# Attention block after group norm: the last output projections in two parts, conversions on ScalarE, residuals one chain ahead

## The chip, the cores and the metric

The kernel runs on one core of a Trainium2 chip as one launch. The metric is the device time of one execution in microseconds (us); lower is better. The five engines run their own instruction queues in order[...]: PE (TensorE, matrix products), ACT (ScalarE), DVE (VectorE), POOL (GpSimd) and SP (SyncE, which here issues nearly all DMAs).

## The reference: what is computed

The input x is 4 images of 512 channels by 48x48 = 2304 positions, in float32. The rest is one self-attention block with a residual:

```python
hn = group_norm(x)                         # 32 groups of 16 channels, per image
qkv = einsum('oc,bchw->bohw', qkv_w, hn) + qkv_b      # 1536 x 512 weights
q, k, v = split(qkv.reshape(b, 3, 8, 64, 2304).astype(float16))
w = softmax(einsum('bhct,bhcs->bhts', q * scale, k * scale))
a = einsum('bhts,bhcs->bhct', w, v).astype(float32)
out = einsum('oc,bchw->bohw', proj_w, a) + proj_b     # 512 x 512 weights
return x + out
```

## The kernel before

**Units.** Of the two paths in the file only `fast_path` runs (`general_path` is entered if the softmax sums leave a safe range; a flag that the fast path computes at its end decides it). The 8 heads of an image are taken as 4 pairs, so there are 16 pairs g = 0..15, four for each image b. The 2304 positions are cut into five blocks j (`QBLOCKS`): four of 512 and one of 256. For each pair and block the keys are gone through in steps; one step k covers three sets of score matrices (`BURST = 3`) and is called an *item* here. A 512-block has six items, the 256-block three, a pair 27, the whole kernel 432 (`stream`, numbered n = 0..431 below).

**An item.** The main loop at the end of `fast_path` takes the items in order. It issues the scores of item n (PE, line 902, into three PSUM banks pairs of the pool `ps_s`), three exponentials of 128x1024 (ACT, line 909), the running sum of the exponentials of item n-1 (DVE, `add`, line 960), and the product with v of item n-2 (PE, line 927; `BEHIND = 2`). When a block is complete, PE adds up the softmax sums (`add_up`, line 980), DVE copies them out (990), SP sends them to another layout (`sums`, 994), DVE inverts them (1025), SP writes the inverse to DRAM (1027) and spreads it back over the partitions (1037), and POOL multiplies (`divide`, 1044). The result `att` is float16.

**Work beside the stream.** Everything else is cut into pieces that are put into one list, `beside`, in an order written out by hand: chains of matmuls that make q and k (`qk_chain`, 704), v (`v_chain`, 749) and the output projection (`proj_pieces`, 829). A chain fills one PSUM bank; all chains share the single bank of the pool `ps_w`, so DVE must empty it (713, 757, 849) before the next chain's matmuls may start. `fill(n)` issues pieces once for each item. How many it may issue is ruled by a credit that is raised by the work left over the items left up to the pair that needs it, and a piece waits in the list until its item `after` has come (`put_convert` and `put_proj`, with `ready` items after the end of the block). Pieces never overtake each other. Because the loop runs when the program is built, the result is a fixed order of instructions on each engine.

**Projection.** For a block of an image the four att tiles are first converted to float32 (`att32`: POOL, line 823; DVE for the last two blocks of the last pair), into one buffer for each of four chunks (`a32_0` to `a32_3`). Then for each 128 output channels one chain runs: four pairs times two halves of the weights (`whi`, `wlo`), eight matmuls into the shared bank. The 256-block has two chains of sixteen. DVE adds bias and the residual x (849), into the tile r that SP loaded (`residual`, 799), and SP stores it (856) one item later. r has three buffers (tag `res`); the load for chain k+1 is a piece of its own ahead of chain k.

**Images.** The projection of image b runs during the pairs of image b+1; that of the last image begins during the last pair, and its last two blocks with a part of the third run after the last item. Tiles of the normed x of the next image are loaded into the buffers of the present one as they come free (`reload`), with statistics and normalization as DVE tasks (`tasks`, up to two or four for each item, `do_tasks`). One block, (1, 3), has buffers elsewhere (`SPARE`) and is loaded early.

Of the kernel before, what the change touches and what calls it, by code (L numbers as in the profile page):

```python
# [467 lines left out]
def fast_path(  # L468
# [13 lines left out]

    const = ctx.enter_context(tc.tile_pool(name="const", bufs=1))
# [3 lines left out]
    apool = ctx.enter_context(tc.tile_pool(name="apool", bufs=8))  # L487
# [12 lines left out]
    SPARE = (1, 3)  # L500

    def load_x(b, j, c, engine):

        o, n = QBLOCKS[j]
        name = f"x_{b}_{c}_{j}"
        if (b, j) == SPARE:
            t = work.tile([P, n], F32, tag=f"a32_{c}", bufs=1, name=name)
        else:
            t = xpool.tile([P, n], F32, tag=f"x{c}_{j}", name=name)
        engine.dma_start(t, x[b, bass.ts(c, P), o : o + n])  # L510
        hn[b, c, j] = t
# [45 lines left out]
    def load_wproj(c):  # L557
        wproj[c] = work.tile([P, C], F32, tag="res", bufs=3, name=f"wproj_{c}")
        nc.sync.dma_start(wproj[c], proj_wT[bass.ts(c, P), :])
# [15 lines left out]
    fine = const.tile([P, 2, QB // P], F32, name="fine")  # L575
# [6 lines left out]
    def chain_bank(name):  # L582
        if alone[0]:
            return ps_s.tile([P, 2, QB], F32, tag="ps", name=name)[:, 0, :]
        return ps_w.tile([P, QB], F32, tag="pw", name=name)
# [202 lines left out]
    def residual(b, j, chunks):  # L788
        n = QBLOCKS[j][1]
        if at_end(b, j):  # L790

            tag = f"x{chunks[0]}_{j - NQ + 2}"
            xt = xpool.tile([P, QB], F32, tag=tag, name=f"r_{b}_{j}_{chunks[0]}")
        else:
            xt = work.tile(
                [P, QB], F32, tag="res", bufs=3, name=f"r_{b}_{j}_{chunks[0]}"
            )
# [4 lines left out]
    def at_end(b, j):  # L802

        return b == B - 1 and j >= NQ - 2

    def att32(b, j, pairs=range(NC)):
        o, n = QBLOCKS[j]
        if (b, j) not in at32:
            if at_end(b, j):
                at32[b, j] = [  # L810
                    xpool.tile([P, n], F32R, tag=f"x{c}_{j}", name=f"a32_{b}_{j}_{c}")
                    for c in range(NC)
                ]
            else:
                at32[b, j] = [
                    work.tile(
                        [P, QB], F32R, tag=f"a32_{c}", bufs=1, name=f"a32_{b}_{j}_{c}"
                    )[:, :n]
                    for c in range(NC)
                ]  # L820
        for c in pairs:
            engine = nc.vector if direct(b * NPAIR + c, j) else nc.gpsimd
            engine.tensor_copy(at32[b, j][c], atts[b * NPAIR + c][:, o : o + n])  # L823

    def proj_chain(b, j, m, ps):
        n = QBLOCKS[j][1]
        for c in range(NC):
            for i, w in enumerate((whi, wlo)):
                nc.tensor.matmul(  # L829
                    ps[:, :n],  # L830
                    w[:, c, bass.ts(m, P)],
                    at32[b, j][c],
                    start=(c == 0 and i == 0),
                    stop=(c == NC - 1 and i == 1),
                )

    def proj_pieces(b, j):


        n = QBLOCKS[j][1]  # L840

        def run(chunks):
            bank = chain_bank(f"pr_{b}_{j}_{chunks[0]}")
            places = [bank[:, i * n : (i + 1) * n] for i in range(len(chunks))]
            for m, ps in zip(chunks, places):
                proj_chain(b, j, m, ps)
            xt = res.pop((b, j, chunks[0]))
            for i, m in enumerate(chunks):
                nc.vector.scalar_tensor_tensor(  # L849
                    xt[:, i], places[i], bproj[:, m : m + 1], xt[:, i], ALU.add, ALU.add  # L850
                )

            loads.append(
                (
                    now[0] + 1,
                    lambda: nc.sync.dma_start(rows_of(out, b, j, chunks), xt),
                )
            )

        def ahead(k):  # L860
            if k < len(proj_list) and not at_end(b, proj_list[k][0]):
                residual(b, *proj_list[k])

        convert = [
            piece(0.0, lambda: att32(b, j, (NC - 1,) if at_end(b, j) else range(NC)))
        ]
        chains = []
        for k, (jj, chunks) in enumerate(proj_list):
            if jj != j:
                continue  # L870
            chains.append(
                [piece(0.0, lambda k=k: ahead(k)) for k in ([0] if k == 0 else [])]
                + [piece(0.0, lambda k=k: ahead(k + 1))]
                + [piece(QB / 290.0, lambda chunks=chunks: run(chunks), True, True)]
            )
        return convert, chains
# [35 lines left out]
    def values(u):  # L912
# [21 lines left out]
        if last:  # L934
            avx[g, j] = work.tile([P, QB], F32, tag="avx", name=f"avx_{g}_{j}")
            nc.vector.tensor_copy(avx[g, j][:, :n], av[0][:, :n])  # L936

    def direct(g, j):

        return g == NG - 1 and j >= NQ - 2  # L940

    def add(u):
# [6 lines left out]
        if direct(g, j) and (last or j == NQ - 1):  # L949
# [16 lines left out]
    def add_up(g, j):  # L966
# [3 lines left out]
        sl = ps_av.tile([P, QB], F32, tag="av", name=f"sl_{g}_{j}")  # L970
# [6 lines left out]
        for i, (t, r, a) in enumerate(steps):  # L977
            for h in range(2):
# [7 lines left out]
                )  # L986

        def rows():
            sx = work.tile([P, QB], F32, tag="rows", name=f"slx_{g}_{j}")
            nc.vector.tensor_copy(sx[:, :n], sl[:, :n])  # L990

            sm = small.tile([P, 2, QB // P], F32, tag="sums", name=f"sums_{g}_{j}")
            for h in range(2):
                nc.sync.dma_start(sm[:, h, : n // P], sx[h * D : h * D + 1, :n])
            sums[g, j] = sm
            return sx

        if direct(g, j):
            source = rows() if n == QB else sl
            inv = work.tile([P, QB], F32, tag="rows", name=f"inv_{g}_{j}")  # L1000
            nc.vector.reciprocal(inv[:, :n], source[:, :n])
            engine = nc.vector if source is sl else nc.gpsimd
            engine.tensor_tensor(
                atts[g][:, o : o + n], avx.pop((g, j))[:, :n], inv[:, :n], ALU.mult
            )
            if source is sl:
                rows()
        else:
            rows()

    def check_sums(g, j):
        n = QBLOCKS[j][1]
        sm = sums[g, j][:, :, : n // P]
        ok = fine[:, :, : n // P]
# [44 lines left out]
    def put_run(run, *args, when=None):  # L1059

        put([piece(0.05, lambda: run(*args), when=when)])

    def reload(b, j):


        def run():
            load_block(b, j)
            for c in range(NC):
                tasks.append((now[0] + 3, lambda c=c: stats(b, j, c)))
            if j == NQ - 1:  # L1070

                tasks.append((now[0] + 3, lambda: aggregate(b)))
                tasks.append((now[0] + 3, lambda: group_scale(b)))
                tasks.append((now[0] + 3, lambda: coefficients(b)))
                for jj in range(NQ):
                    for c in range(NC):
                        tasks.append((now[0] + 3, lambda jj=jj, c=c: normalize(b, jj, c)))
# [7 lines left out]
    def do_tasks(room):  # L1085
# [3 lines left out]
        while tasks and tasks[0][0] <= n and room > 0:  # L1089
            tasks.popleft()[1]()  # L1090
            room -= 1
# [18 lines left out]
    def ready(b, j):  # L1110
# [3 lines left out]
        return BEHIND + (2 if j >= NQ - 2 else 5)  # L1114
# [5 lines left out]
    def put_proj(b, j, *which):  # L1120

        end = ends[((b + 1) * NPAIR - 1) * NQ + j]
        for i in which or range(len(projs[b, j][1])):
            put(projs[b, j][1][i], end + ready(b, j) + 1)

    for b in range(B):
        g = b * NPAIR
        old = b - 1
        if b == 0:
# [7 lines left out]
            put_run(reload, *SPARE)  # L1137
        put_qk(g + 2, 1)
        put_qk(g + 2, 0)

        late = SPARE[1] if b == 0 else None
        last_tiles = [i for i in range(0, NT, 2) if i * P // QB == late]
        put_v(b, 1, [i for i in range(0, NT, 2) if i not in last_tiles])
        if b == B - 1:
            put_qk(g + 3, 1)
            put_qk(g + 3, 0)
            put_convert(old, 0)
            for j in range(NQ):
                put_proj(old, j)
                if j + 1 < NQ:  # L1150
                    put_convert(old, j + 1)
            for j in range(NQ - 2):
                put_convert(b, j)
                put_proj(b, j)
                if j < 2:
                    for jj, chunks in proj_list:
                        if jj == NQ - 2 + j:
                            put_run(residual, b, jj, chunks)
                    put_run(att32, b, NQ - 2 + j, range(NC - 1))
            put_convert(b, NQ - 2)  # L1160
            put_proj(b, NQ - 2)
            continue

        for j in range(NQ):
            if j == late:
                continue
            if j == 3 and b > 0:
                put_convert(old, 0)
# [3 lines left out]
        if late is not None:  # L1172
            put_v(b, 1, last_tiles)
            put_qk(g + 3, 1, (late,))
            put_qk(g + 3, 0, (late,))
# [55 lines left out]
    def fill(n):  # L1231
# [6 lines left out]
        do_tasks(  # L1238
            (2 if idle else 0)
            if ended(n - 1)  # L1240
            else (2 if idle else 1) if ended(n - BEHIND - 1) else 4 if idle else 2
        )
        rate, work = 0.0, 0.0
        for us, _, _, _, _, _, need in beside:
            work += us
            left = min(need * per_pair, len(stream)) - n
# [12 lines left out]
    def wanted(g):  # L1259

        while any(p[6] <= g for p in beside):
            while loads:
                loads.popleft()[1]()
            while tasks:
                tasks.popleft()[1]()
# [4 lines left out]
    end = len(stream)  # L1270
    for n in range(end):
# [103 lines left out]
```

## Time and profile before

| What | us |
|---|---|
| Median of 3 runs (lowest to highest) | 1649.59 (1648.8 to 1651.96) |
| The profiled execution, its own time | 1654.24 |
| Its span, from first to last instruction | 1652.5 |
| Start of the first item's scores | 80.6 |
| Start of item 395 (the last chain that makes q) | 1484.1 |
| Start of the scores of the last item | 1621.98 |
| End of the last exponential | 1625.3 |
| End of the last DVE addition | 1645.8 |

The profiled execution is one run; its time is 4.65 us above the median of the timed runs, of which 1.74 us lie outside its span. Sums are made inside the span and carried over to the median as a difference. The mean granted clock of TensorE is 0.996 of full speed. Busy times of PE count matmuls that overlap, with modelled ends, so idle PE time in a busy column understates waiting; the starts of the instructions do not have that fault, and stretches are measured by them.

### The profile page before, as it was taken

The page shows a single profiled execution, that of the slowest core. Times are in us where ns is not written, and L with a number is a line of the kernel's source. Part 1 is how long each engine was busy: PE and PEld are TensorE (multiplying, and loading weights), DVE is VectorE, ACT ScalarE, POOL GpSimd, SP SyncE. Part 2 cuts the span into 40 slices and gives each one's busy share as a digit, 9 for nine tenths or more (in the row PEclk, how much of TensorE's full clock was granted, in tenths as well). Part 3 has the DMA queues.
Part 4 walks back from the last instruction along what each step waited for, and adds up shares of the span by engine and source line. Part 5 has one row for each costly group of instructions (what it writes and reads, how often), then busy time and mean ns, then how long its engine had stood idle before and what let it go on. Part 6 is the DMA issues. An engine that isn't in the chain of part 4 may idle for free.

```text
span 1652.5 us, 28302 instructions
## 1 busy us (share of the span) xinstructions
PE 1591.0 (96%) x11500; PEld 695.2 (42%) x11500; DVE 1137.5 (69%) x1296; ACT 1247.7 (76%) x1317; POOL 372.1 (23%) x497
## 2 busy tenths in 40 slices
PE   6999999899999999899999999899999999999887
PEld 2533444343333534445333353345533334435445
DVE  5267668876666679786666666788667666767664
ACT  3077777788888888678887888667878888887772
POOL 1001111222121223413212121332211122214341
PEclk9999999999999999999999999999999999999999
DMA  7001012000000015421000001342100000013443
GB/s 217 1 14 40 11 40 71 17 14 11 14 18 14 15 36 147 120 70 37 14 15 11 14 18 55 109 132 74 37 14 11 14 17 15 15 29 107 134 122 124
DMA packets 95185, 82.11 MB, mean 50 GB/s; under 512 B 51140, under 2 KB 61252, under 8 KB 95044
## 3 DMA queue, kind: packets, MB, share of 16 engines
q1 hardware_dynamic: 93572, 79.14, 17.3%
q8 instruction: 92, 1.51, 0.4%
q10 hardware_dynamic: 1344, 1.05, 0.2%
q14 instruction: 49, 0.40, 0.1%
q0 software_dynamic: 128, 0.01, 0.0%
HBM read 60.70 MB, written 19.17 MB: 48 GB/s over the span
## 4 chain that ended last, share of the span: by engine, by line
PE 86%; DMA 5%; DVE 4%; POOL 2%; issue 2%; ACT 1%; SPq 1%; DVEq 0%; POOLq 0%
PE pqk L704 28%; PE ps L902 17%; PE av L927 17%; PE pv L749 15%; PE pr L829 6%; DMA out_dram<-r 2%; DVE acc L960 1%; PE ps L704 1%; PE sl L980 1%; POOL a L823 1%; DMA r<-x_dram 1%; ACT p L909 1%; DMA ib<-row 1%; DMA x<-x_dram 1%; DMA sums<-slx 1%
## 5 line engine op out<-in xcount | busy, mean ns | idle before, releaser
L909 ACT ACTIVATE p<-ps 128x1024 f16<-128x1024 f32 x1296 | 1232.7, 1027 | 361.9 <-PE ps L902 361.1
L960 DVE TENSOR_TENSOR acc<-acc,p 128x3072 f16<-128x3072 f16 x270 | 486.9, 1803 | 75.8 <-ACT p L909 75.4
L704 PE MATMUL pqk<-x,wqkv 128*64 128x512 f32 (+1 forms) x2464 | 519.3, 551 | 0.0
L902 PE MATMUL ps<-q,k 64*128 64x512 f16 (+1 forms) x2880 | 360.7, 359 | 10.8 <-ACT p L909 10.4
L927 PE MATMUL av<-p,v 128*64 128x512 f16 (+1 forms) x2880 | 360.7, 364 | 0.0
L1018 POOL TENSOR_SCALAR in<-sums 128x8 f32<-128x8 f32 (+1 forms) x160 | 121.3, 758 | 716.0 <-DMA sums<-slx 709.3
L749 PE MATMUL pv<-wqkv,x 128*64 128x256 f32 x2304 | 268.9, 380 | 4.3 <-DVE x L655 2.7
L704 PEld LDWEIGHTS pqk<-x,wqkv 128*64 128x64 f32 x2464 | 169.1, 137 | 223.5 <-issue 166.6
L1044 POOL TENSOR_TENSOR att<-avx,ib 128x512 f16<-128x512 f32 (+1 forms) x78 | 131.2, 1683 | 447.3 <-DMA ib<-row 396.9
L902 PEld LDWEIGHTS <-k 64*128 64x128 f16 x2880 | 106.6, 94 | 293.1 <-issue 246.4
L927 PEld LDWEIGHTS <-v 128*64 128x64 f16 x2880 | 131.7, 109 | 209.8 <-issue 164.8
L749 PEld LDWEIGHTS pv<-wqkv,x 128*64 128x64 f32 x2304 | 160.3, 137 | 97.5 <-issue 5.5
L829 PE MATMUL pr<-a,whi 128*128 128x512 f32 (+1 forms) x320 | 127.2, 405 | 23.1 <-DVE r L849 11.3
L960 DVE TENSOR_TENSOR acc<-p,p 128x3072 f16<-128x3072 f16 x79 | 138.2, 1749 | 0.0
L963 DVE TENSOR_TENSOR acc<-acc 128x1024 f16<-128x1024 f16 x156 | 115.3, 739 | 5.3
L829 PE MATMUL pr<-a,wlo 128*128 128x512 f32 (+1 forms) x320 | 118.4, 378 | 0.0
L713 DVE TENSOR_SCALAR q<-pqk,bqkv 128x512 f16<-128x512 f32 (+1 forms) x79 | 55.0, 696 | 86.6 <-PE pqk L704 86.3
L757 DVE TENSOR_TENSOR v<-pv,bv 128x512 f16<-128x512 f32 x72 | 49.8, 691 | 79.5 <-PE pv L749 79.2
L713 DVE TENSOR_SCALAR k<-pqk,bqkv 128x512 f16<-128x512 f32 (+1 forms) x75 | 52.2, 695 | 72.0 <-PE pqk L704 71.9
L849 DVE SCALAR_TENSOR_TENSOR r<-pr,bproj,r 128x512 f32<-128x512 f32 (+1 forms) x80 | 54.9, 694 | 61.9 <-PE pr L829 43.3
L936 DVE COPY avx<-av 128x512 f32<-128x512 f32 (+1 forms) x80 | 51.0, 637 | 66.8 <-PE av L927 66.5
L829 PEld LDWEIGHTS pr<-a,whi 128*128 128x128 f32 x320 | 60.9, 190 | 65.1 <-POOL a L823 23.1
(51 smaller groups left out, 453.3 us busy)
## 6 DMA issues: line engine op xcount, KB each, us to landing
r<-x_dram SPq DMA_DIRECT2D x72, 256.0 KB, 3.0
out_dram<-r SPq DMA_DIRECT2D x72, 256.0 KB, 3.1
ib<-row SPq DMA_DIRECT2D x126, 128.0 KB, 3.0
x<-x_dram SPq DMA_DIRECT2D x62, 256.0 KB, 4.4
x<-x_dram SPq DMA_DIRECT2D x16, 128.0 KB, 4.6
sums<-slx SPq DMA_DIRECT2D x128, 2.0 KB, 2.0
ib<-row SPq DMA_DIRECT2D x30, 64.0 KB, 2.9
wqkv<-qkv_wT_dram SPq DMA_DIRECT2D x2, 768.0 KB, 6.9
```

What stands on the lines that cost most here:

```text
L704: nc.tensor.matmul(pw[0][lo : lo + D, :n], wqkv[:, c, w0 + lo : w0 + lo + D], hn[b, c, j], start=(c == 0), stop=(c == NC - 1),)
L713: nc.vector.tensor_scalar(qk[g][part][:, o : o + n], pw[0][:, :n], bqkv[:, col : col + 1], SCALE, ALU.add, ALU.mult,)
L749: nc.tensor.matmul(pw[0][lo : lo + D, a, :], hn[b, c, i * P // QB][:, at + lo : at + lo + D], wqkv[:, c, 2 * C + half * C // 2 :][:, : C / ...
L829: nc.tensor.matmul(ps[:, :n], w[:, c, bass.ts(m, P)], at32[b, j][c], start=(c == 0 and i == 0), stop=(c == NC - 1 and i == 1),)
L849: nc.vector.scalar_tensor_tensor(xt[:, i], places[i], bproj[:, m : m + 1], xt[:, i], ALU.add, ALU.add)
L902: nc.tensor.matmul(ps[:, h, a * n : (a + 1) * n], kt[rows, bass.ts(i, P)], qt[rows, o : o + n], start=True, stop=True,)
L909: nc.scalar.activation(pt[:, r], ps, AF.Exp)
L927: nc.tensor.matmul(av[0][lo : lo + D, :n], vv[b, pr // 2][:, i, pr % 2 * P + lo : pr % 2 * P + lo + D], pt[:, r, h, a * n : (a + 1) * n], ...
L960: nc.vector.tensor_tensor(t, before, pt, ALU.add)
L963: nc.vector.tensor_tensor(t[:, 0], t[:, 0], t[:, r], ALU.add)
L1018: nc.gpsimd.tensor_scalar(t, sm, limit, None, op)
L1044: nc.gpsimd.tensor_tensor(atts[g][:, o : o + n], avx.pop((g, j))[:, :n], ibs.pop((g, j))[:, :n], ALU.mult,)
```

## The change

It has five parts.

1. **Last image in two parts.** For the blocks j = 2, 3, 4 of the last image the projection over the first three head pairs (`FIRST`) is put into the list beside the last pair's items; DVE adds it and the bias into r. The fourth pair's share (`LAST`) is added by a second chain of two matmuls for each 128 channels: block 2 and the blocks 3 and 4 after the last item. The residuals of these blocks are loaded into x tiles during the projection of image 2.
2. **Order of the end.** The blocks that end at items 422 and 428 are added up in the same turn in which their last products are issued, and the 256-block's sums and division are written out behind the loop; its check runs on all 128 x 256 sums on POOL. Stores alternate between the queues of SP and ACT. Of the 256-block the product with v stays in PSUM.
3. **Conversion on ScalarE.** `att32` copies with ACT instead of POOL.
4. **Residuals.** r has four buffers, and the load for chain k+1 is issued with chain k instead of as a piece ahead of it; the load for chain 0 goes with the conversion.
5. **Next image's x.** Two blocks of image 1, (1, 2) and (1, 3), are preloaded, the first into the four `res` buffers; the order of chains around them follows. DVE tasks are allowed by time (0.5 to 2.4 us for each item) instead of by number, and the pace of pieces reckons with two items fewer.

```diff
-    SPARE = (1, 3)
+    SPARE = {(1, 2): lambda c: ("res", RES), (1, 3): lambda c: (f"a32_{c}", 1)}
...
     def residual(b, j, chunks):
-        if at_end(b, j):
-            tag = f"x{chunks[0]}_{j - NQ + 2}"
+        if in_two(b, j):
+            tag = f"x{chunks[0]}_{(j - NQ + 2) % 3}"
             xt = xpool.tile([P, QB], F32, tag=tag, name=f"r_{b}_{j}_{chunks[0]}")
         else:
             xt = work.tile(
-                [P, QB], F32, tag="res", bufs=3, name=f"r_{b}_{j}_{chunks[0]}"
+                [P, QB], F32, tag="res", bufs=RES, name=f"r_{b}_{j}_{chunks[0]}"
             )
...
+    def in_two(b, j):
+        return b == B - 1 and j >= NQ - 3
+
+    def left_over(b, j):
         return b == B - 1 and j >= NQ - 2
...
-        for c in pairs:
-            engine = nc.vector if direct(b * NPAIR + c, j) else nc.gpsimd
-            engine.tensor_copy(at32[b, j][c], atts[b * NPAIR + c][:, o : o + n])
+            at32[b, j, c] = t[:, :n]
+            nc.scalar.copy(at32[b, j, c], atts[b * NPAIR + c][:, o : o + n])
...
+    FIRST, LAST = range(NC - 1), range(NC - 1, NC)
+
+    def proj_run(b, j, chunks, pairs=range(NC), bank=None):
+        n = QBLOCKS[j][1]
+        if bank is None:
+            bank = chain_bank(f"pr_{b}_{j}_{chunks[0]}")
+        places = [bank[:, i * n : (i + 1) * n] for i in range(len(chunks))]
+        for m, ps in zip(chunks, places):
+            proj_chain(b, j, m, ps, pairs)
+        xt = res[b, j, chunks[0]]
+
+        def evacuate():
+            if pairs == LAST:
+                ps = bank[:, : len(chunks) * n].rearrange("p (m n) -> p m n", n=n)
+                nc.vector.tensor_tensor(xt, ps, xt, ALU.add)
+            else:
+                for i, m in enumerate(chunks):
+                    bias = bproj[:, m : m + 1]
+                    nc.vector.scalar_tensor_tensor(
+                        xt[:, i], places[i], bias, xt[:, i], ALU.add, ALU.add
+                    )
+
+        def store(engine=nc.sync):
+            engine.dma_start(rows_of(out, b, j, chunks), xt)
+
+        return evacuate, store
+
+    def proj_piece(b, j, chunks, pairs=range(NC), ahead=None):
+        def run():
+            if ahead is not None:
+                ahead()
+            evacuate, store = proj_run(b, j, chunks, pairs)
+            evacuate()
+            if pairs != FIRST:
+                loads.append((now[0] + 1, store))
+
+        return piece(QB / 290.0 * len(pairs) / NC, run, True, True)
...
-                tasks.append((now[0] + 3, lambda c=c: stats(b, j, c)))
+                tasks.append((n, 0.65, lambda c=c: stats(b, j, c)))
...
-        return BEHIND + (2 if j >= NQ - 2 else 5)
+        return BEHIND + 5
...
             for j in range(NQ):
-                put_proj(old, j)
+                put_proj(old, j, ahead)
                 if j + 1 < NQ:
                     put_convert(old, j + 1)
-            for j in range(NQ - 2):
-                put_convert(b, j)
-                put_proj(b, j)
-                if j < 2:
-                    for jj, chunks in proj_list:
-                        if jj == NQ - 2 + j:
-                            put_run(residual, b, jj, chunks)
-                    put_run(att32, b, NQ - 2 + j, range(NC - 1))
-            put_convert(b, NQ - 2)
-            put_proj(b, NQ - 2)
+                if j >= NQ - 2:
+                    there = ends[(NG - 2) * NQ + j] + BEHIND + 6
+                    put_run(att32, b, j, FIRST, after=there)
+            put_first(b, NQ - 2)
+            put_run(att32, b, NQ - 3, FIRST)
+            put_first(b, NQ - 3)
+            put_convert(b, 0)
+            put_proj(b, 0)
+            put_first(b, NQ - 1)
+            put_convert(b, 1)
+            put_proj(b, 1)
+            put_convert(b, NQ - 3)
+            put_proj(b, NQ - 3)
             continue
...
-            left = min(need * per_pair, len(stream)) - n
+            left = min(need * per_pair, len(stream) - BEHIND) - n
...
+    soon = ends[-3:-1]
...
+        if n - BEHIND in soon:
+            g, j = stream[n - BEHIND][:2]
+            sx = rows(g, j, add_up(g, j))
+            if n - BEHIND == soon[1]:
+                divide_here(g, j, sx, avx[g, j], nc.gpsimd)
...
+    check_sums(g, NQ - 2)
+    att32(b, NQ - 2, LAST)
+    add(stream[-1])
+    values(stream[-1])
+    sl = add_up(g, j, small_bank("sl_last"))
...
+    divide_here(g, j, sl, av[0], nc.vector)
+    att32(b, j, LAST)
     alone[0] = True
...
+    rest = [(jj, chunks) for jj, chunks in proj_list if left_over(b, jj)]
+    ends_of = []
+    for i, (jj, chunks) in enumerate(rest):
+        if i % 2 == 0:
+            banks = ps_s.tile([P, 2, QB], F32, tag="ps", name=f"rest_{i}")
+        ends_of.append(proj_run(b, jj, chunks, LAST, banks[:, i % 2, :]))
...
+    for i, (evacuate, store) in enumerate(ends_of):
+        if i == NC - 1:
+            nc.vector.tensor_reduce(good, fines, AX.X, ALU.add)
+            nc.tensor.matmul(pf, good, ones, start=True, stop=True)
+        if i == len(rest) - 1:
+            nc.vector.tensor_scalar(flag, pf, P * every - 0.5, None, ALU.is_lt)
+        evacuate()
+        store(nc.scalar if i % 2 else nc.sync)
```

## The prediction

> **What bounds the kernel now.** I read the shares of busy time first, then the waits, then windows of the span (busy time of each engine), and last the order in time of single items.
>
> ```profile
> PE 1591.0 (96%) x11500; PEld 695.2 (42%) x11500; DVE 1137.5 (69%) x1296; ACT 1247.7 (76%) x1317; POOL 372.1 (23%) x497
> ```
>
> ```profile
> PE pr L829 <- DVE r L849: 11.3, 8, 5.2
> PE ps L902 <- ACT p L909: 10.4, 22, 0.5
> PE pr L829 <- POOL a L823: 8.7, 11, 2.3
> ```
>
> PE is the bound on the whole. The waits (line waited at, total, times, longest) say where it isn't: at projection chains that wait for the residual addition (L849) or for POOL's conversion (L823), and at scores that wait for exponentials. To see where, I take an item's PE work from start-to-start times: scores 0.75, values 0.67, half a q or k chain 1.77, half a v chain 1.78, a projection chain 2.06, softmax sums 0.32. Items 2 to 58, 62 to 157, 192 to 270 and 312 to 395 take 1.0% more than that sum (209.0 us for 206.9 in the first). These have nothing to win. What is left:
>
> ```profile
> 295.27:311.86 16.59, 11.08 (x84) 4.46 (x83) 15.00 (x31) 11.16 (x13) 3.60 (x6) 1.00 0.06 9
> 639.84:775.48 135.64, 128.34 (x993) 69.73 (x992) 106.97 (x140) 100.03 (x106) 44.74 (x53) 1.00 0.32 92
> 1043.93:1209.48 165.55, 156.15 (x1120) 78.15 (x1118) 124.28 (x159) 119.95 (x127) 45.94 (x57) 0.98 0.30 85
> 1484.10:1621.98 137.88, 122.54 (x757) 61.06 (x756) 90.06 (x90) 102.10 (x109) 53.72 (x69) 0.99 0.43 129
> 1621.98:1652.50 30.52, 22.60 (x176) 18.71 (x174) 14.47 (x21) 2.86 (x3) 3.05 (x9) 0.95 0.29 99
> ```
>
> Columns: window, length, then busy us of PE, PEld, DVE, ACT, POOL, then granted clock. In order: A, items 58 to 62, work 9.6; B, 157 to 192, work 124.8; C, 270 to 312, work 149.2; D, 395 to 431, work 112.6; and the tail. With 1% allowed, A loses 6.9, B 9.6, C 14.9 and D 24.2. An undisturbed projection item takes 3.58 for 3.49 of work, 0.06 beyond the 1%; for the 18 and 20 of B and C that is 1.1 and 1.2 that no change here removes, which leaves 8.5 to win in B and 13.7 in C.
>
> Why: SP's waits show the residual's load (L799) behind the landing of an older store, since r has three buffers and the load for chain k+1 precedes the store of chain k-1; in C one wait of 5.3 us has the load queued behind four x loads.
>
> ```profile
> SPq L799 <- DMA out_dram<-r: 127.2, 48, 5.3
> ...
> DVE r L849 <- DMA r<-x_dram: 13.5, 7, 6.1
> ```
>
> In D eight items have no work beside the stream (399, 415 to 417, 422, 423, 428, 429). Such an item runs at ACT's pace: three exponentials take 2.76 where PE has 1.42. The scores below wait for ACT each time:
>
> ```profile
> 1612.84 0.39 PE L902 MATMUL ps<-q,k 64*128 64x256 f16 x4
> 1613.73 0.39 PE L902 MATMUL ps<-q,k 64*128 64x256 f16 x4 [0.51 <-ACT p L909]
> 1614.65 0.39 PE L902 MATMUL ps<-q,k 64*128 64x256 f16 x4 [0.52 <-ACT p L909]
> ```
>
> In a projection item (3.58 from scores to scores) the exponentials take 2.85, so ACT idles 0.72:
>
> ```profile
> 1583.81 0.82 PE L902 MATMUL ps<-q,k 64*128 64x512 f16 x6
> 1584.30 2.85 ACT L909 ACTIVATE p<-ps 128x1024 f16<-128x1024 f32 x3 [0.78 <-PE ps L902]
> 1587.39 0.82 PE L902 MATMUL ps<-q,k 64*128 64x512 f16 x6
> ```
>
> **The change, part by part.** PE's total work is the same; it is only placed elsewhere. How the changed kernel's instructions follow each other gives the places.
>
> *Next image's x (window A).* The second spare block lets v chains start without the wait for x of 2.83; items 58 to 61 all get beside work. A goes from 16.6 to 9.7: -6.9. The loads are hidden: the DMA share is 0.06 there. If a load is late, PE waits at its first v chain, at most the 6.9 again.
>
> *Residuals (B, C).* Load k+1 is issued with chain k into the buffer of chain k-3, whose store was issued two items (7.2 us) earlier and lands in some 3.1 us; it also leaves the place behind x loads. The gain is the wait at L849, and with POOL's conversions gone all excess of B and C: -8.5 and -13.7. SP issues as many DMAs as before; what queues behind a load there are sums and row transfers of the divide, which now wait less.
>
> *Conversion on ScalarE.* POOL loses 63 casts of 0.935. ACT gains them, four in a row, after the exponentials of items 155, 160, 164, 168 and 172 for image 0, five such places for images 1 and 2, and smaller groups for the last. A copy waits for att, long finished, save at item 430, where block 2's division leaves an estimated margin of 5 us. It is not free on ACT: behind the copies stand the next item's exponentials, behind these the scores that need the PSUM banks, behind these all of PE. The trace of before has no copy on ACT. The nearest row is the normalization of the first x tiles,
>
> ```profile
> 11.84 3.43 ACT L662 ACTIVATE x<-x,gb,ga 128x512 f32<-128x512 f32 x5 [5.70 <-DVE gb L648]
> ```
>
> five in 3.43, start to start 0.705, with two per-partition operands (ga, gb). [...] Four take 4 x 0.52 + 0.09 = 2.17. ACT's idle time of 0.73 hides part; the scores may lag 0.75 more before PE stands, because the third exponential ends at 1587.15 and its bank is wanted at 1587.90. The stall is 2.17 - 0.73 - 0.75 = 0.69 in a projection item and 1.36 after an item of 3.24 (155, 271, 393), where ACT has 0.67 less to spare. In B: 1.36 + 3 x 0.6 (the fifth copies only 256 columns) = 3.3 with rounding; C the same. In D: 1.36 at 393, 2.0 at the next four places of image 2, 2.8 at the groups of three for FIRST (411 to 420), whose items have less PE work, 1.5 at 426: 7.6. Sum 14.2. At the row's 0.705 four take 2.92, each stall grows by 0.75, and the sum is 26.5; with stalls absorbed by the slack of following items, about 6.
>
> [...] The trace's one 128x512 cast of att on DVE took 0.418 against 0.52, and DVE idles as well. [...]
>
> So B: -8.5 + 3.3 = -5.2; C: -13.7 + 3.3 = -10.4. With A: -22.5.
>
> *The last image (D and the tail).* Three quarters of three blocks' projection move beside items that were bare. D's PE work rises from 112.6 to 124.3, and 1.8 of work is drawn to before item 395. D: 124.3 x 1.01, plus 34 projection items x 0.06, is 127.6; plus 7.6 is 135.2 against 137.9: -2.7, with +1.8 before it. The tail begins at the last scores, T. Before, PE had 24.4 of work there. After, it has 10.9: scores, values and the last exponentials to T+3.55, sums of 36 matmuls (2.1) to T+5.65, DVE's inverse of the 256 block (1.76) and multiplication (0.42) to about T+7.95, then two-matmul chains that PE finishes faster than DVE empties: ten evacuations by some 0.67 (0.75 with two operands and bias before) and the reduction, to T+15.0. The end lies 6.7 behind the last addition (1645.8 to 1652.5: flag, branch, closing), and I take 6.5 to 6.7. The tail becomes 21.6 for 30.5: -8.9. Alternate stores on ACT's queue are hidden by DVE's chain, as ACT has no exponentials left; if the last store lands later than the flag's branch, at most some 2 us return.
>
> *DVE's tasks by time, and the pace:* no price of their own. DVE is 69% busy, and the statistics lie in undisturbed stretches, at 1% excess. If a task delays an evacuation, a chain waits for its bank, at the most the 0.65 of one task; bounds -2 to +3.
>
> Sum: -22.5 + 1.8 - 2.7 - 8.9 = -32.3. The span goes from 1652.5 to 1620, and the median from 1649.6 to 1617, the execution profiled being 4.65 above the median both times.
>
> **The rivals.**
>
> *Copies absorbed.* PE work in later items and exponentials that run ahead take up the stalls: 14.2 falls to 6 or less, and part of the 1% excess goes. -40 to -45: 1607. For it: ACT is at 76%. Against it: a projection item leaves it only 0.72.
>
> *ACT limits the projection.* The copy costs 0.705 or more, with stalls of 26.5 in place of 14.2: -20, 1630. For it: the only row. Against it: that row has two operands more.
>
> *A wait persists.* The change doesn't do what it says: residuals are still late, as each passes SP's queue behind waits for rows (140 us at L1037), or DVE's evacuation comes late. Half of B and C and some of D are lost: -10, 1640.
>
> *Slower.* Copies at the head of ACT's queue hold the exponentials so long that all is lost: the gain without stalls is 32.3 + 14.2 = 46.5, over 15 groups of four and the smaller ones (four more such groups), so it decides at 2.45 us for each group beyond what is hidden, with 1.48 hidden 3.9 for four, or about 0.96 a copy. POOL's cast is that slow (0.935), but with DVE in its way; ACT's row at 0.705 speaks against it. Price at 1.2 a copy: 4.8 - 1.48 = 3.3, by 19 = 63: +17, 1666.
>
> **How the numbers follow.** Likeliest 0.50 at 1617 (own range 1611 to 1624); absorbed 0.20; ACT limits 0.20; a wait persists 0.06; slower 0.03; no change 0.01. No more than 2 in 10 is left out between 1603 and 1632: the ends are the absorbed case's -46 and the row's 0.705 with 2 on top. A measurement of this kernel tells 0.2% (3.3 us) from nothing. Faster 0.95, within 0.02, slower 0.03.
>
> **What would show it.** The changed profile should have no wait of PE for a conversion on POOL, SP's wait of the residual for a store near zero, no row of scores with 256 columns waiting three times for ACT in D, scores after a group of copies late by 0.7 to 1.4, a copy of 128x512 starting 0.52 after the one before, the last scores at about 1621.98 - 22.5 + 1.8 - 2.7 = 1598.6, and the last addition 15 behind them. The prediction is wrong if the copy takes above 0.7, if B and C still hold waits at residual additions, or if the last additions wait for something other than DVE.

## The result, and the profile after

The changed kernel takes 1635.38 us in the median of four runs (1634.64 to 1636.16), the kernel before 1650.59 beside it: a ratio of 0.9909, with a 95% interval of 0.9891 to 0.9926. It is faster by 15 us, where 33 were forecast, and lies 3.4 us outside the stated range. In a later comparison it stood at 0.9899 (0.9881 to 0.9917), 17 us below. The profiled executions differ by 18.2: 1634.3 for 1652.5 us of span.

Shares of busy time on the page of the changed kernel, then waits of PE and DVE, then SP's (line waited at, what for, total us, times, longest):

```profile
PE 1586.6 (97%) x11500; PEld 696.5 (43%) x11500; DVE 1135.6 (69%) x1302; ACT 1284.2 (79%) x1398; POOL 301.2 (18%) x419
```

```profile
DVE r L858 <- DMA r<-x_dram: 10.9, 5, 4.3
...
PE pr L831 <- ACT a L825: 7.3, 3, 3.0
...
PE pr L831 <- DVE r L858: 6.1, 8, 1.7
...
PE ps L924 <- ACT p L931: 5.1, 12, 0.5
```

```profile
SPq L1044 <- DVE inv L1042: 253.0, 76, 5.3
...
SPq L863 <- DVE r L858: 55.2, 28, 5.2
```

POOL has lost its casts. SP's wait of the residual's load for an older store (127 us before) no longer stands in the list. But PE still waits for conversions, now on ACT, in three places of up to 3.0 us, and still for residual additions (L858); and the additions still wait for their loads, 10.9 us for 13.5 before. The windows (window, length, busy us of PE, PEld, DVE, ACT, POOL, granted clock) of the same items as before, A, B, C, D and the tail:

```profile
294.11:309.05 14.94, 14.94 (x132) 7.59 (x131) 12.30 (x16) 11.47 (x13) 1.87 (x5) 1.00 0.05 10
635.22:766.51 131.29, 126.33 (x968) 68.65 (x967) 105.03 (x137) 108.49 (x123) 29.09 (x33) 1.00 0.34 95
1034.97:1189.67 154.70, 151.06 (x1110) 76.77 (x1109) 121.15 (x156) 128.60 (x147) 31.67 (x41) 1.00 0.31 91
1466.16:1611.43 145.27, 133.62 (x804) 72.15 (x803) 92.79 (x100) 119.34 (x144) 25.41 (x31) 0.98 0.42 121
1611.43:1634.30 22.87, 10.79 (x112) 8.35 (x110) 12.63 (x16) 4.25 (x6) 4.72 (x9) 0.86 0.37 132
```

D is the surprise: 145.3 us, longer than the 137.9 of before. Some 11.7 us more of PE work were placed in it; the time beyond its work, 25.3 us before and forecast to be 10.9, is 21.0. Its clock is 0.98, the tail's 0.86. Since work moves between windows, kernels are compared below by the *excess* of a stretch: its time from start to start less the PE work of its items.

In order of time, ACT and PE in item 403, which has the first chain of block 2 of image 2:

```profile
1498.08 2.85 ACT L931 ACTIVATE p<-ps 128x1024 f16<-128x1024 f32 x3 [1.42 <-PE ps L924]
1498.41 0.84 PE L949 MATMUL av<-p,v 128*64 128x512 f16 x6
...
1500.81 2.18 ACT L825 CAST a<-att 128x512 fp32r<-128x512 f16 x4
1501.49 0.79 PE L831 MATMUL pr<-a,whi 128*128 128x512 f32 x1 [2.25 <-ACT a L825]
1502.09 0.63 PE L831 MATMUL pr<-a,wlo 128*128 128x512 f32 x1
1502.51 0.63 PE L831 MATMUL pr<-a,whi 128*128 128x512 f32 x1
...
1505.40 0.83 PE L924 MATMUL ps<-q,k 64*128 64x256 f16 x12
```

The four copies were issued in the same item as the chain that reads them. They stand behind that item's three exponentials, and PE waits 2.25 us for the first. Four copies in 2.18 are 0.515 from start to start, as forecast. The next matmuls start 0.43 apart, where 0.235 is usual. The windows around it show why:

```profile
1498.00:1499.20 1.20, 1.20 (x16) 0.44 (x10) 1.20 (x2) 1.12 (x2) 0.00 (x0) 1.00 0.69 260
1499.20:1501.40 2.20, 0.05 (x2) 0.00 (x0) 0.80 (x2) 2.20 (x4) 0.00 (x0) 1.00 0.50 149
1501.40:1503.00 1.60, 1.51 (x4) 1.22 (x5) 0.00 (x0) 1.60 (x4) 0.00 (x0) 0.51 0.80 287
1503.00:1505.00 2.00, 2.00 (x6) 1.26 (x4) 0.00 (x0) 0.00 (x0) 0.00 (x0) 0.54 0.00 0
1505.00:1508.00 3.00, 3.00 (x23) 2.04 (x22) 2.83 (x3) 2.17 (x3) 0.00 (x0) 1.00 0.01 0
```

After the wait the granted clock is half for some 3.4 us (1.6 us at 0.51 and 2.0 at 0.54). Item 403 takes 7.75 us for 3.81 of work. Item 407 takes 8.05 for 3.49: PE waits 3.02 us there, and the half clock begins some 1.4 us after the wait. In item 411 PE waits 2.04 and the clock stays at 1.00: 5.94 for 3.52. Together the three lose 10.9 us.

In item 407 a second cause lies just beneath the first. The shared bank came free only when DVE had made an addition that waited 4.29 us for its residual, some 0.7 us before the first copy was done:

```profile
1519.01 0.75 DVE L858 SCALAR_TENSOR_TENSOR r<-pr,bproj,r 128x512 f32<-128x512 f32 x1 [4.29 <-DMA r<-x_dram]
...
1519.84 2.19 ACT L825 CAST a<-att 128x512 fp32r<-128x512 f16 x4
...
1520.53 0.50 PE L831 MATMUL pr<-a,whi 128*128 128x512 f32 x1 [3.02 <-ACT a L825]
```

### The profile page after: what moved, and what is told of

It reads as the page before. It is cut to its first block, busy times and chain, and to the rows that moved or that the text cites. A ratio compares the mean times of both kernels' runs of the same rounds, so it can differ in the third digit from the quotient of the medians.

```text
span 1634.3 us, 28292 instructions
## 1 busy us (share of the span) xinstructions
PE 1586.6 (97%) x11500; PEld 696.5 (43%) x11500; DVE 1135.6 (69%) x1302; ACT 1284.2 (79%) x1398; POOL 301.2 (18%) x419
## 4 chain that ended last, share of the span: by engine, by line
PE 88%; DVE 4%; ACT 3%; DMA 3%; issue 1%; SPq 0%; DVEq 0%; ACTq 0%
PE pqk L709 29%; PE ps L924 18%; PE av L949 18%; PE pv L754 15%; PE pr L831 5%; ACT p L931 3%; DMA r<-x_dram 2%; PE ps L709 1%; DVE acc L978 1%; PE sl L1000 1%; DVE r L858 1%; ACT a L825 1%; DMA x<-x_dram 1%; DVE inv L1023 0%; DVE r L854 0%
## 5 line engine op out<-in xcount | busy, mean ns | idle before, releaser
L1035 POOL TENSOR_SCALAR in<-sums 128x8 f32<-128x8 f32 (+1 forms) x158 | 110.5, 700 | 800.9 <-DMA sums<-slx 794.5
L831 PE MATMUL pr<-a,whi 128*128 128x512 f32 (+1 forms) x312 | 123.5, 403 | 13.8 <-ACT a L825 7.3
L981 DVE TENSOR_TENSOR acc<-acc 128x1024 f16<-128x1024 f16 x156 | 109.3, 701 | 5.3
L858 DVE SCALAR_TENSOR_TENSOR r<-pr,bproj,r 128x512 f32<-128x512 f32 (+1 forms) x80 | 54.9, 695 | 65.7 <-PE pr L831 46.7
L831 PEld LDWEIGHTS pr<-a,whi 128*128 128x128 f32 x312 | 59.1, 189 | 52.4 <-issue 15.4
```

Source lines behind the costliest of these rows:

```text
L831: nc.tensor.matmul(ps[:, :n], w[:, c, bass.ts(m, P)], at32[b, j, c], start=(i == 0), stop=(i == len(steps) - 1),)
L858: nc.vector.scalar_tensor_tensor(xt[:, i], places[i], bias, xt[:, i], ALU.add, ALU.add)
L981: nc.vector.tensor_tensor(t[:, 0], t[:, 0], t[:, r], ALU.add)
L1035: nc.gpsimd.tensor_scalar(t, sm, limit, None, op)
```

## The experiments

Excess in us by stretch, from one profiled execution each, and the tail from the last item's scores to the end (the kernel before and the changed kernel were profiled twice, for the scatter):

| kernel | A, 58 to 62 | B, 157 to 192 | C, 270 to 312 | D, 395 to 431 | tail | span |
|---|---|---|---|---|---|---|
| before | 7.0 / 7.0 | 10.8 / 9.5 | 16.3 / 16.2 | 25.3 / 26.9 | 30.5 / 31.1 | 1652.5 / 1652.6 |
| changed | 0.1 / 0.1 | 8.3 / 9.8 | 7.3 / 6.2 | 21.0 / 20.5 | 22.9 / 23.1 | 1634.3 / 1634.7 |
| e1_early | 0.1 | 10.2 | 7.6 | 12.5 | 23.0 | 1628.5 |
| e2_pool | 0.1 | 8.8 | 11.1 | 13.3 | 23.1 | 1632.3 |
| e3_two_ahead | 0.1 | 5.3 | 5.0 | 20.2 | 24.2 | 1630.7 |
| e5_early_two | 0.1 | 5.7 | 5.0 | 9.7 | 23.5 | 1618.8 |
| e6_dve | 0.1 | 5.9 | 4.9 | 6.9 | 23.5 | 1616.4 |
| e4_split | 0.1 | 4.2 | 4.2 | 5.3 | 23.6 | 1613.0 |
| e9_double | 0.1 | 15.4 | 18.5 | 32.7 | 23.1 | 1670.1 |
| e11_before_res | 7.1 | 8.9 | 13.8 | 21.0 | 35.4 | 1647.7 |

My theory after the traces: D fails because three conversions stand in the item of their first chain; B because residuals are still late; the price of a copy was right. The rivals: ACT has no room for the copies at all, or DMA decides in D too.

**Conversions an item earlier** (e1_early). A free piece is issued although the credit is negative.

```diff
-            if credit[0] < us / 2:
+            if us > 0.0 and credit[0] < us / 2:
                 break
             issue()
```

> The changed kernel, but a conversion of price nothing is issued even when the credit is negative: the three conversions of image 2 that stood in the fill of the same item as the first chain that reads them (items 403, 407, 411) go one item earlier (402, 406, 410). Nothing else moves. Theory 1 (in those items PE waited for a copy that stands behind the item's three exponentials on ACT's queue; excess 3.84 + 4.46 + 2.3 = 10.6 us in the changed kernel's trace, clock loss after the wait included): the excess falls to what the other conversions show (0.5 to 0.7 each), so about -8.6 us against the changed kernel, near 1627. Theory 2 (ACT has no room for the copies, wherever they stand): no more than -2 us. Theory 3 (residuals or DMA load in that region): no change.

Measured: 1630.95, ratio 0.9864 (0.9849 to 0.9879), against 0.9899 for the changed kernel beside a run of before. D's excess falls by 8.0 to 8.5, as expected; the time gains only 5.4 to 6, short of the 8.6 expected, and the profiled execution has 0.4 to 1.9 more excess in B and 0.3 to 1.4 more in C than the changed kernel's two, where nothing was changed. With the conversions out of the way the residuals are what is late: the additions wait for their loads for longer than in the changed kernel, four times in items 407 to 411.

```profile
DVE r L858 <- DMA r<-x_dram: 19.7, 10, 3.1
```

The chain of item 403 now follows without a gap; the copies stand ahead of the exponentials of that item, which start late instead:

```profile
1499.14 2.19 ACT L825 CAST a<-att 128x512 fp32r<-128x512 f16 x4
...
1499.57 0.83 PE L924 MATMUL ps<-q,k 64*128 64x256 f16 x12
...
1501.21 1.04 ACT L931 ACTIVATE p<-ps 128x1024 f16<-128x1024 f32 x1
1501.26 0.47 PE L831 MATMUL pr<-a,whi 128*128 128x512 f32 x1
```

Theory 2 falls with it: the same copies cost ACT the same time in both. So does theory 3 as the main cause in D, since no transfer was moved.

**Conversions back on POOL** (e2_pool).

```diff
-            nc.scalar.copy(at32[b, j, c], atts[b * NPAIR + c][:, o : o + n])
+            nc.gpsimd.tensor_copy(at32[b, j, c], atts[b * NPAIR + c][:, o : o + n])
```

> The changed kernel with the conversions back on POOL, in the same places of the order. Theory 1: a cast on POOL doesn't stand behind the exponentials, so items 403, 407 and 411 lose only what four casts of 0.94 take beyond the cover (1 to 2 us each instead of 3.84, 4.46, 2.3), the stalls of exponentials by copies (157, 273, 395, 418, 422, 428: about 1.1 each) go, and waits for POOL of the size before (8.7 us) come back elsewhere: within 4 us of the changed kernel. Rival (the move to ScalarE is itself the gain in the projection stretches): slower than the changed kernel by 8 us or more.

Measured: 1635.57, ratio 0.989 (0.9875 to 0.9906), the same as the changed kernel. As placed, the move to ScalarE is worth nothing: what it gains in C (11.1 to 7.3 and 6.2) it loses in D (13.3 to 21.0 and 20.5), and the rival is out. Whether POOL would fall behind once conversions and residuals are early was not run. POOL's casts are as slow as they were, 0.942 us in the mean for 0.935:

```profile
L825 POOL CAST a<-att 128x512 fp32r<-128x512 f16 x64 | 58.0, 942 | 52.9 <-PE pr L831 47.0 <-PE pqk L709 5.9
```

**Residuals two chains ahead** (e3_two_ahead).

```diff
             if j == 0:
                 ahead(0)
+                ahead(1)
...
-            proj_piece(b, j, chunks, pairs, lambda k=k: ahead(k + 1))
+            proj_piece(b, j, chunks, pairs, lambda k=k: ahead(k + 2))
```

> The changed kernel with the residual for chain k+2 (instead of k+1) issued with chain k. Theory (one chain ahead is still too late where SP's queue is held up by stores that wait for DVE and by x loads): the waits of the residual addition for its load (10.9 us in 5 places) go, and PE's excess at items 164, 167 and 276 (1.67, 0.74, 1.75) with them: -3 to -4 us against the changed kernel. Rival (the buffer of chain k-2 isn't free yet, so the load waits for that store's landing and holds up SP's queue): 0 to +4.

Measured: 1631.26 (1627.22 to 1632.53), ratio 0.9855 (0.984 to 0.987), 5 to 7 below the changed kernel; B loses 5.3 for 8.3 and 9.8, C 5.0 for 7.3 and 6.2. No wait of the residual addition for a load is left among the listed ones; in the changed kernel one was

```profile
664.32 0.75 DVE L858 SCALAR_TENSOR_TENSOR r<-pr,bproj,r 128x512 f32<-128x512 f32 x1 [2.48 <-DMA r<-x_dram]
```

and its load came late because of what stands ahead of it on SP's queue (start and length of SP's instructions, same kernel):

```profile
654.56 0.43 SPq L804 DMA_DIRECT2D r<-x_dram  x1
658.88 0.38 SPq L1044 DMA_DIRECT2D row<-inv  x1
659.31 0.47 SPq L863 DMA_DIRECT2D out_dram<-r  x1
659.82 0.43 SPq L804 DMA_DIRECT2D r<-x_dram  x1
```

The row transfer of a division waited 3.9 us for DVE's inverse, and the next load behind it started 5.3 us after the one before, not 3.6. It landed at about 664.3, 4.5 us after its start, where the median on the page is 3.4 for such a load; the DMA engines were busy for 0.93 of the time from 662 to 664. By these figures the queue made it some 1.7 us late, and the transfer itself about 1. In C (item 276) four x loads stand ahead of the residual's instead. The rival fails: SP's loads wait 10.6 us for stores, but two chains early.

**The residuals' part alone, on the kernel before** (e11_before_res: four buffers, the load for chain k+1 issued by chain k, seven att buffers for eight to make room).

```diff
-                [P, QB], F32, tag="res", bufs=3, name=f"r_{b}_{j}_{chunks[0]}"
+                [P, QB], F32, tag="res", bufs=4, name=f"r_{b}_{j}_{chunks[0]}"
...
-        def run(chunks):
+        def run(chunks, k):
+            ahead(k + 1)
```

> The kernel before with the residuals' part of the change alone: four buffers, the load for chain k+1 issued with chain k, that for chain 0 with the conversion (one of the eight att buffers is given up for the room). Theory 1 (what was lost to residuals was the load's wait for the store of three chains before): SP's wait of the load for a store (127 us) goes, and the excess of items 157 to 192 and 270 to 312 falls from 10.8 and 16.3 by 8 in all, the rest being waits for POOL's casts; about -8 us. Theory 2 (the lead of one chain, behind stores that wait for DVE and x loads, is what is short): the waits of the residual addition for its load stay near 11 to 14 us, and the gain is 0 to -4.

Measured: 1647.88 for 1654.0 (0.9958, 0.994 to 0.9977), -6. SP's wait for older stores is gone, B and C fall only by 3 to 4.5 of the 25.7 to 27.1, and the additions wait longer for their loads than the 13.5 us of before:

```profile
DVE r L850 <- DMA r<-x_dram: 18.4, 7, 4.5
```

So theory 2 holds for B and C. D gains 4 to 6, for a reason that stays open, so that the whole gains more than the 0 to 4 of theory 2; the tail gives back 4 to 5, which may be the missing att buffer (not tried apart).

**Both edits, copies on ACT** (e5_early_two).

> The changed kernel with the two earlier edits together (conversion of image 2 an item earlier, residuals two chains ahead), all copies on ACT. It leaves only the halving of the copies on ACT between this and e4_split. If the edits add up: -8.5 for the one and -5 for the other against the changed kernel, -13.5; and then the division of the copies between ACT and DVE is worth about -9 (e4_split stands about 22 below the changed kernel by the traces). Rival (the division is worth little, and the two edits help each other): within 3 us of e4_split.

Measured: 1620.47 for 1653.42, ratio 0.98 (0.9783 to 0.9818): -33.0 against before, -15.9 against the changed kernel beside it (-13.5 expected). They do more than add up (5.4 to 6 and 5 to 7 alone): in D the earlier conversions bring out the late residuals, and the earlier residuals remove them (excess 12.5 with the first edit, 9.7 with both). The rival had half of this right, but e4_split is more than 3 us away. Of the excess left in B, C and D (5.7, 5.0, 9.7) the division below takes out 6.7; about half of the rest is the 0.1 us or less of each item in which nothing waits.

**Copies on DVE** (e6_dve, the same with the tensor copy of DVE).

> The two edits, with all four copies of a group on DVE (0.418 each by the trace of before, four 1.7) and none on ACT. Theory (each engine hides about 1.5 us beside a projection item; what matters is the length of the queue in front of the exponentials): no exponential waits behind a copy, but the next running sum of DVE and the evacuation of the next chain stand 1.7 late behind four casts; DVE has some 1.0 us of idle time in a projection item, and an evacuation 0.75 of slack: 0 to +3 against e4_split. Rival (DVE's additions become the bound): +8 or more against e4_split.

Measured: 1618.16, ratio 0.979 (0.9772 to 0.9807), about 2 below the copies on ACT and 4 to 5 above the division between both (the next run): somewhat over what was expected, and short of the rival. A cast of 128x512 on DVE takes 0.434 in the mean.

**Copies divided** (e4_split). Pairs 0 and 2 on ACT, 1 and 3 on DVE, with both edits.

```diff
-            nc.scalar.copy(at32[b, j, c], atts[b * NPAIR + c][:, o : o + n])
+            engine = nc.vector.tensor_copy if c % 2 else nc.scalar.copy
+            engine(at32[b, j, c], atts[b * NPAIR + c][:, o : o + n])
```

> Both of these (conversion an item earlier, residual two chains ahead), and of each group of four copies pairs 1 and 3 on DVE, 0 and 2 on ACT. Theory 1: -8.6 for the three items, -3.5 for the residuals, and the exponentials' stalls behind four copies (1.29, 1.09, 1.33 at items 157, 273, 395, about 1.0 at 418, 422, 428) shrink as two copies take 1.13 against 0.73 idle and 0.75 slack: -4 to -5. Together -16 against the changed kernel, near 1619. Rival (DVE's casts delay its additions and evacuations by as much): -10 to -12.

Measured: 1614.23 (1613.63 to 1615.25), ratio 0.9759 (0.9746 to 0.9773), the fastest of all: some 40 below before, 22 to 23 below the changed kernel (-16 expected; the two edits together made up the difference). The division alone is worth 6 to 7 (against e5_early_two; 9 was expected there). What is left of the waits for conversions and residuals:

```profile
PE pr L832 <- DVE r L859: 2.9, 7, 0.8
...
PEld pr L832 <- ACT a L826: 1.7, 4, 0.4
```

**Every copy twice on ACT** (e9_double, on e5_early_two).

```diff
             nc.scalar.copy(at32[b, j, c], atts[b * NPAIR + c][:, o : o + n])
+            nc.scalar.copy(at32[b, j, c], atts[b * NPAIR + c][:, o : o + n])
```

> The kernel of e5_early_two with every copy on ACT issued twice, so that a group of four takes 4.2 us in place of 2.2: it measures what a microsecond in front of the exponentials costs. Theory (ACT's 0.73 of idle time and 0.75 of PSUM slack are used up by the first 1.5 us, and every further microsecond is lost to PE): 14 groups of four x 2.06, two of three x 1.55 and the 256-column ones some 2 in all, +34 against e5_early_two, near 1654. Rival (later items make up for it, as most groups in images 0 and 1 showed only 0 to 0.7 of stall): +20 or less.

Measured: 1671.23, ratio 1.0098 (1.0067 to 1.0129), +49 to +51 against e5_early_two: above the theory's 34, and far from the rival. The 80 copies more are some 38 us of ACT's time (64 of 512 columns at 0.515, 16 of 256 at about 0.3). Scores wait for 25.4 us, where e5_early_two has 5.4:

```profile
PE ps L926 <- ACT p L933: 25.4, 43, 2.4
```

The mean granted clock is 0.992, against 0.998 in e5_early_two. In item 157, after such waits, projection matmuls start 0.43 apart, as in item 403 above. An estimate from clocks and spans: 0.008 of 1670 us is lost to the lower clock, and 0.002 of 1619 in e5_early_two, so the clock makes at most 10 of the 51. What is left, some 41, is about the length of the copies: once the slack was used, a microsecond ahead of the exponentials cost PE about a microsecond here (41 for 38), and the lower clock came on top. Some 7 beyond the theory's 34 and the clock's 10 stay unexplained.

**The changed kernel and the kernel before again** (e7_changed, e8_before).

> The changed kernel itself, on the same chip as these, so that differences are taken between kernels that share their runs of the kernel before: ratio 0.991 as before; by stretches the same trace to within 2 us, except where a DMA's landing decides (B and C).

> The kernel before, profiled a second time. If its profiled execution was slow by chance (4.65 us over the median), the excess of items 157 to 173 and 270 to 290, where the residuals' landings decide, is less than 8.2 and 15.3 by 3 to 4 us in all, and the rest is the same to 0.3. If not, both are as before.

Measured: 1636.36 (0.9899) and, by the one execution, 1654.37. The stretches repeat within 1.6 us in both, and before's excess in B and C is hardly smaller (25.7 for 27.1). So the profiled execution of before was not an odd one; its runs scatter more (1648.8 to 1659.9 over all comparisons) than those of the changed kernel (1634.6 to 1638.3).

## Why the prediction was right or wrong

| step | predicted | measured | |
|---|---|---|---|
| start, before item 58 | 0 | -1.2 | -0.7 of it before the first item, where the profiled executions scatter by 1.5 |
| A | -6.9 | -7.0 | right |
| B | -5.2 | -2.6 | residuals still late; +0.3 by the second pair of profiles |
| C | -10.4 | -9.1 | nearly right |
| work drawn ahead of item 395 | +1.8 | +1.8 | right |
| D | -2.7 | +7.4 | conversion and chain in one item |
| tail | -8.9 | -7.7 | DVE and the closing later |
| span | -32.3 | -18.2 | |

The rows A to C are changes of excess, those of D and the tail changes of length, from one profile of each kernel.

**A** is right to 0.1: every item has work beside the stream, and no v chain waits for x. The window itself lasts 14.9 us and not the 9.7 of the forecast, since 5.3 us of PE work came into it, which later windows no longer have.

**The price of the copy** is right too. No row of before shows the 0.52 a copy and the 0.09 beside it of which the forecast made 2.17 for four, and from them its stalls: they were the author's assumption. The changed kernel's trace has 0.515 from start to start, 0.63 for a copy alone and 2.18 for four, and not the 0.705 of the nearest row. The stall of 0.69 behind four copies in a projection item was 0.55 (the usual 0.1 taken off) at items 283, 287 and 400 of the changed kernel and 1.0 at 422 and 428; elsewhere late residuals hide it, or it is smaller. That of 1.36 after a shorter item was 1.2, 1.0 and 1.2 at 157, 273 and 395. The rival in which ACT is the limit by its copies' length is out, and so is the one in which they are absorbed.

**D** is the step that failed. It said "The stall is 2.17 - 0.73 - 0.75 = 0.69 in a projection item and 1.36 after an item of 3.24", for every group, and counted 2.0 for the next four places of image 2. The formula holds where the chain comes an item later. At items 403, 407 and 411 the chain is in the same item, so PE waits for the exponentials in front of the copies as well, and in two of the three for its clock afterwards: 10.9 us, where the forecast had 2.0 for four places. The order of the instructions showed this, and I read from it only after which exponentials the copies stand, not which item reads them first. Moving these three conversions alone took 8 us out of D (excess 21.0 and 20.5 to 12.5). In item 407, by the lines shown above, the late residual would have held PE nearly as long; but in e3_two_ahead, where no residual is late, item 407 still takes 7.95 us, so the conversion is enough by itself.

**B** fell short at "with POOL's conversions gone all excess of B and C: -8.5 and -13.7". I priced the wait of a load for an old store, which did go, and missed that SP's queue in front of the load holds a division's transfer and a store that wait for DVE. The forecast looked at what queues behind a load ("which now wait less") and not at what stands ahead of it. SP's waits at these two lines, 253.0 and 55.2 us in the changed kernel, were in the profile of before too:

```profile
SPq L1027 <- DVE inv L1025: 233.6, 74, 5.3
...
SPq L856 <- DVE r L849: 24.8, 16, 5.4
```

I had named that as a rival, "a wait persists", at 0.06. Loading two chains ahead took another 3 to 4.5 out of B and 1 to 2 out of C. The "one wait of 5.3 us" in C was misread: SP's longest wait for a store lies in D, and in C PE waited 5.2 us for an addition whose load followed four x loads.

**The tail** was forecast 1.3 too short: the multiplication of the last block was done at T+9.7, not 7.95. The sums began at T+4.85, not 3.55; 1.0 of that is a wait for an addition that DVE made after its inverse of 3.35 us. The inverse of the last block began another 0.5 after the sums' end, behind ACT's copy of them, which the forecast left out:

```profile
1612.33 3.35 DVE L1023 RECIPROCAL inv<-slx 128x512 f32<-128x512 f32 x1
...
1615.60 0.63 DVE L854 TENSOR_TENSOR r<-pr,r 128x512 f32<-128x512 f32 x1
...
1616.28 2.15 PE L1000 MATMUL sl_last<-p,ones 128*64 128x256 f16 x36 [1.03 <-DVE r L854]
...
1618.94 1.76 DVE L1023 RECIPROCAL inv<-sl_last 128x256 f32<-128x256 f32 x1 [2.72 <-ACT fines L1370]
```

Shorter evacuations (0.63) made most of that good, to T+15.75 for 15.0; the closing took 7.1 for 6.6.

**From span to median**: "the execution profiled being 4.65 above the median both times" failed; the changed kernel's was 0.66 above. The span shrank by 18.2 and the median by 15.2 and 17.1 in the two comparisons.

Mechanism and sum come close in e5_early_two, where those three conversions and the residuals are in time, as the forecast took them to be: it stands 33.0 below before, and the forecast was 32.3. That is not one lucky sum: B gains 5.1 (5.2 forecast), C 11.3 (10.4), D's window 3.9 (2.7) and the tail 7.1 (8.9). But it needed loads two chains ahead, and the forecast had held one to be enough.

Of the two engines alone, DVE was the better place with both edits: all copies on DVE were some 2 us faster than all on ACT (1618.16 for 1620.47), 0.434 us a cast where ACT's copies start 0.515 apart. But neither end is best. Half on each (1614.23) is 4 to 5 below DVE alone.

## What to carry to other kernels

A step moved to another engine cost here only its length past the idle time and buffer slack of that engine where its reader came later than the work queued in front of it (0.55 us for four copies of 2.18 at items 283, 287 and 400); where the reader came first, it cost that work as well (3.9 us at item 403, half clock included). So check in the built order which item issues it and which item first reads it. A load that is "one step ahead" is as early as the oldest waiting instruction in front of it on its queue lets it be (here a row transfer that waited 3.9 us made the next load some 1.7 late), so count the queue and not the steps. Short work put ahead of a nearly full engine may be worth dividing over two engines, each within its own slack: here that was the fastest of the three ways tried with both edits (1614.23 us, for 1618.16 on DVE and 1620.47 on ACT).

## What was not expected of the hardware

A wait of 2.25 us on PE was followed by half the clock for 3.4 us, which nearly doubled its price: item 403 lost 3.9 us. It isn't the wait's length alone. The chain of item 409 in the kernel before shows both cases, in its two profiled executions. In the first PE waited 2.26 us and went on at the full clock; in the second it waited 1.90 us, and the clock was half for 3.4 us soon after (the first matmul after the wait in each, then a window of each, with the granted clock third from the end):

```profile
1540.84 0.50 PE L829 MATMUL pr<-a,whi 128*128 128x512 f32 x1 [2.26 <-POOL a L823]
...
1538.31 0.50 PE L829 MATMUL pr<-a,whi 128*128 128x512 f32 x1 [1.90 <-POOL a L823]
```

```profile
1540.84:1544.24 3.40, 3.40 (x18) 1.60 (x20) 0.95 (x2) 0.62 (x1) 1.63 (x3) 1.00 0.11 41
...
1539.00:1542.40 3.40, 3.40 (x11) 1.83 (x12) 0.66 (x1) 0.12 (x1) 0.93 (x2) 0.50 0.00 0
```

In item 407 of the changed kernel, too, the clock was half for 3.4 us (from 1521.9 to 1525.3), after a wait of 3.02. So its two stretches at half clock were equally long, and the waits before them were not. What decides whether the clock drops after such a wait, and when, no run here shows.
